# The first expert layer of nineteen late slots, computed from quarter blocks with seven products

## The chip, the cores and the metric

The kernel runs on one core of one Trainium2 chip. The metric is the device time of one execution in microseconds; 893.2 us is the median of seven runs before the change (892.81 to 895.32). The core has five engines with a queue each: PE (matrix products, with its weight loads shown apart as PEld), DVE (vector), ACT (activation), POOL (GpSimd) and SP (issues transfers). All arithmetic is in 32-bit floats.

## The reference

A layer norm, a cross attention with 16 heads onto 64 context rows per batch, a gated residual, a second layer norm, and a mixture of 8 experts of which each of the 4096 tokens uses two:

```python
x = x + tanh(g_xattn) * attention(layernorm(x), ctx, ctx)
# the experts, on xt = layernorm(x), 4096 x 256
logits = einsum('td,ed->te', xt, gate_w)
w_topk, sel = top_k(logits, 2)
combine = zeros((T, E)).at[arange(T)[:, None], sel].add(softmax(w_topk))
h = silu(einsum('td,edf->tef', xt, w1))      # first layer, 256 -> 1024
y = einsum('tef,efd->ted', h, w2)            # second layer, 1024 -> 256
x = x + tanh(g_ffn) * einsum('ted,te->td', y, combine)
```

## The kernel before, in words

The attention runs over eight groups of 512 tokens. After the second layer norm every token is written twice, once for each chosen expert, into a table in device memory that is sorted by expert. The experts are then computed in "slots": a slot is a stretch of table rows of one expert. Nine early slots (0 to 8, `NA` = 9) take rows of the first four groups and run while the attention of the rest goes on. Late slots begin at 9. The first eight of them (9 to 16, `NW` = 8) are three blocks of 128 rows wide, so 384 rows; the others (17 on) have two blocks, 256 rows. This execution computes slots 0 to 29.

`run_slots` is the loop over slots. For slot `s` it runs `hidden` (L842: the first layer), then `transposed` for slot `s + 1` (L832: DVE turns the rows into columns, `xT`), then `combine` (L942: the second layer) of slot `s - 1`, then `quarter_sums` of slot `s` (L878), and asks for the weights of slot `s + 3` and the rows of slot `s + 4`. So the second layer runs one slot behind the first. In what follows "a first-layer stretch" is the time in which PE computes `hidden` of one slot, and "a second-layer stretch" that of `combine`.

`hidden` multiplies, for each of eight feature blocks of 128, two halves of the 256 inputs (`NC` = 2) by all rows of the slot: 16 products with 384 or 256 columns, added up in PSUM. One instruction of ACT then applies silu to 768 or 1024 columns of PSUM and writes `hT`. DVE has no part in it.

The second layer of slots 9 to 27 (`by_quarters`, L875) is already computed with seven products in place of eight on two by two quarter blocks (a scheme of Strassen and Winograd). `quarter_sums` makes eight sums of 128 x 512 on DVE, four of `hT` and four of `w2`, all with both inputs in SBUF. `pair_of_blocks` (L898) has seven products of four 128 x 128 matmuls and leaves PSUM through ACT (L923, L933) and DVE (L918). A third block is computed the plain way (L987). The scaled rows are added to the output by an indirect transfer that POOL issues (`scatter`, L958).

Names that matter: `block` gives out buffers of 8 KB per partition in three shares, "group" (8), "weight" (7) and "hidden" (2). `w1` and `w2` of even late slots counted from 9 lie in "weight", those of odd ones in "group"; `sh` and `sw` lie in "weight"; `hT` lies in "hidden", or for every second wide slot in "group". `ps2` is two tiles of two PSUM banks each, used by `hidden`; `ps1` is four banks, used by the second layer. `soft` with the tag "pr" is two tiles of 1024 columns. `kept` are the eight residual tiles of the attention; the first two of them are not used by late slots.

The order of instructions on each engine is not that of the source alone: a scheduler at build time issues what it holds to be ready, earlier source first, and each engine then works through its queue strictly in order.

Of the kernel before, what the change touches and what calls it, by code (L numbers as in the profile page):

```python
# [8 lines left out]
F32 = mybir.dt.float32  # L9
I32 = mybir.dt.int32  # L10
AF = mybir.ActivationFunctionType
ALU = mybir.AluOpType
# [3 lines left out]
P = 128  # L16
# [5 lines left out]
def kernel(  # L22
# [36 lines left out]
    nc = tc.nc  # L59
# [3 lines left out]
    H, _, DK = w_qs.shape  # L63
    E, _, F = w1.shape
# [6 lines left out]
    NC = D // P  # L71
    NF = F // P
# [5 lines left out]
    NA = -(-(2 * HG * G - E * (S - 1)) // S)  # L78
# [12 lines left out]
    soft = ctx.enter_context(tc.tile_pool(name="soft", bufs=2))  # L91
# [5 lines left out]
    ps2 = ctx.enter_context(tc.tile_pool(name="ps2", bufs=2, space=PSUM))  # L97
    ps1 = ctx.enter_context(tc.tile_pool(name="ps1", bufs=4, space=PSUM))

    def block(shape, name, share):  # L100
        return blocks.tile(shape, F32, tag=share, bufs=shares[share], name=name)

    def bank(name, spare=False):

        if spare:
            return ps2.tile([P, 2, 512], F32, tag="ps2", name=name)[:, 0]
        return ps1.tile([P, 512], F32, tag="ps1", name=name)
# [3 lines left out]
    of = out.rearrange("b l d -> (b l) d").rearrange("(g t p) d -> g p t d", p=P, t=T)  # L111
# [10 lines left out]
    kept = [const.tile([P, T * RW], F32, tag=f"x{g}", name=f"x{g}") for g in range(NG)]  # L122
# [38 lines left out]
    wk, _ = next(load_wk)  # L161
# [603 lines left out]
    def is_wide(s):  # L765
        return NA <= s < NA + NW
# [15 lines left out]
    def load_tokens(s):  # L782

        blocks = 3 if is_wide(s) else 2
        ids = routed.tile([P, 3, 2, 2], F32, tag="ids", name=f"ids_{s}")[:, :blocks]
        xin = places(s)
        parts = [(1, 0, 2), (2, 2, 3)][: blocks - 1]
        behind = ["cleared", "table0"] if s < NA else ["cleared", "table0", "table1"]
        assert entered >= (HG if s < NA else NG) * T * 2
        for row, first, last in parts:  # L790
            n = (last - first) * P
            with behind_loads():
                r = number(s, row, table_rows - n)
            of = table[bass.ds(r, n), :]
            load = nc.sync.dma_start(
                ids[:, first:last, 0], of[:, 0:2].rearrange("(t p) c -> p t c", p=P)
            )
            apart("table", load, behind=behind)
            with tc.issue_after(load.ins):
                load = nc.sync.dma_start(  # L800
                    ids[:, first:last, 1], of[:, D + 2 : D + 4].rearrange("(t p) c -> p t c", p=P)
                )
            apart("table", load, behind=behind)
            for c in range(P // Q):
                with tc.issue_after(load.ins):
                    load = nc.sync.dma_start(
                        xin[c * Q : (c + 1) * Q, first:last].rearrange("j t (i w) -> j (t i) w", w=D // 4),
                        of[:, 2 + c * (D // 4) : 2 + (c + 1) * (D // 4)].rearrange("(i j) w -> j i w", j=Q),
                    )
                apart("table", load, behind=behind)  # L810
            issued[:] = [load.ins]
        return ids, xin

    def load_weights(s):

        with behind_loads():
            e = number(s, 0, E - 1)
        w = s - NA
        share = "weight" if s < NA or w % 2 == 0 else "group"
        a = block([P, NC, F], f"w1_{s}", share)  # L820
        nc.sync.dma_start(a, w1[bass.ds(e, 1)].rearrange("o (p c) f -> p (o c) f", p=P))
        b = block([P, NF, D], f"w2_{s}", share)
        issued[:] = [
            nc.sync.dma_start(b, w2[bass.ds(e, 1)].rearrange("o (c p) d -> p (o c) d", p=P)).ins
        ]
        return a, b
# [5 lines left out]
    def transposed(s, xin):  # L832
        blocks = xin.shape[1]
        pool, tag = (rows, "xT") if blocks == 2 else (npool, "nT")
        xT = pool.tile([P, NC, blocks * P], F32, tag=tag, name=f"xT_{s}")
        nc.vector.transpose(
            xT.rearrange("p c (i j) -> p i c j", j=Q),
            xin.rearrange("p t (i m c) -> p (t i) c m", c=NC, m=Q),
        )
        return xT  # L840

    def hidden(s, a, xT):  # L842

        n = xT.shape[2]
        if is_wide(s):
            share = "hidden" if (s - NA) % 2 == 0 else "group"
            hT = [block([P, NF // 2, n], f"hT_{s}_{i}", share) for i in range(2)]
        else:
            hT = [block([P, NF, n], f"hT_{s}", "hidden")]
        per_tile = NF // len(hT)  # L850
        step = 4 if attention_ends and not is_wide(s) else 2
        for f0 in range(0, NF, step):
            if not attention_ends:
                ph = bank(f"ph_{s}_{f0}").rearrange("p (i n) -> p i n", i=2)
            elif is_wide(s):
                ph = ps2.tile([P, 2, 512], F32, tag="ps2", name=f"ph_{s}_{f0}")[:, :, :n]
            else:
                ph = ps2.tile([P, step, n], F32, tag="ps2", name=f"ph_{s}_{f0}")
            for i in range(step):
                f = f0 + i  # L860
                for c in range(NC):
                    nc.tensor.matmul(  # L862
                        ph[:, i, :],
                        a[:, c, f * P : (f + 1) * P],
                        xT[:, c, :],
                        start=(c == 0),
                        stop=(c == NC - 1),
                    )
            f1 = f0 % per_tile
            nc.scalar.activation(hT[f0 // per_tile][:, f1 : f1 + step, :], ph, AF.Silu)  # L870
            yield hT

    attention_ends = False

    def by_quarters(s):  # L875
        return NA <= s < NA + OFTEN - 2
# [126 lines left out]
    def run_slots(slots):  # L1003

        ahead = 3
        issued.clear()
        tokens, weights = {}, {}

        def load(s):
            if s in slots:  # L1010
                weights[s] = load_weights(s)

        def load_next(s):
            if s in slots:
                tokens[s] = load_tokens(s)

        for s in slots[:ahead]:
            load(s)
            load_next(s)
        load_next(slots[0] + ahead)  # L1020
        yield
        yield
        xT = transposed(slots[0], tokens[slots[0]][1])
        yield
        pending = None
        for s in slots:
            a, b = weights.pop(s)
            ids, xin = tokens.pop(s)
            if s == slots[-1] and pending:
                yield from combine(*pending)  # L1030
                pending = None
            for hT in hidden(s, a, xT):
                yield
            if s + 1 in slots:
                xT = transposed(s + 1, tokens[s + 1][1])
                yield
            if pending:
                yield from combine(*pending)
            pending = (s, ids, b, xin, hT, quarter_sums(s, b, hT) if by_quarters(s) else None)
            load(s + ahead)  # L1040
            load_next(s + ahead + 1)
        yield from combine(*pending)
# [64 lines left out]


    slots = run_slots(range(NA + OFTEN))
    pieces = {HG + 2: (0, 0, 1, 1), HG + 3: (3, 3, 2, 2), HG + 4: (3, 3, 3, 3)}  # L1110
    last = None
# [13 lines left out]
    for g in range(NG + 1):  # L1125
# [7 lines left out]
        for t in range(T):  # L1133
            if t == 0 and g >= 2:
                leave(g - 2)
            if g < NG:
                pr = probabilities(g, t, qT)
# [44 lines left out]
    for _ in slots:  # L1182
# [3 lines left out]
    _, used = nc.values_load_multi_w_load_instructions(  # L1186
        in_use[0:1, 0:1], min_val=0, max_val=NB, bass_reorder=False
    )
    with tc.If(used[0] > OFTEN):
        for _ in run_slots(range(NA + OFTEN, NA + RARELY)):  # L1190
            pass
        with tc.If(used[0] > RARELY):
            for _ in run_slots(range(NA + RARELY, NS)):
                pass
# [32 lines left out]
```

## Time and profile before

| | |
|---|---|
| median of seven runs | 893.2 us |
| the profiled execution's own time | 893.94 us |
| its span, first to last instruction | 892.2 us |
| busy: PE, DVE, ACT, POOL | 856.0, 451.7, 250.7, 259.8 us |
| first layer of all slots on PE (L862) | 248.1 us |
| second layer by quarters on PE (L908) | 134.4 us (54.0 + 40.1 + 20.2 + 20.1) |
| sums of `quarter_sums` on DVE (L895) | 103.5 us |
| mean granted clock of PE | 0.986 |

The span is what the profile shows between the first and the last instruction; 1.7 us of the execution's own time lie around it. The slots that the change touches are computed between about 542 and 868 us of the span. A matmul of 32-bit floats shows as two records: the 16 products of `hidden` are 32 records per slot. Start times are the best measure of PE's pace, as the ends of matmuls are modelled.

### The profile page before, as it was taken

What the parts mean: (1) busy time and instruction counts of PE and PEld (TensorE: products, weight loads), DVE (VectorE), ACT (ScalarE), POOL (GpSimd) and SP (SyncE); (2) the same over time, 40 slices, a digit from 0 to 9 for tenths busy, and PEclk for the clock granted to TensorE, in tenths of its full rate; (3) what the DMA queues carried; (4) which work ended last, traced back from release to release, by engine and by line L of the source; (5) the groups of instructions that cost most, each with busy time, mean ns of one, the idle gap of its engine ahead of it and who ended that gap; (6) DMA issues with size and microseconds to landing.
All of it is one profiled execution on the core that took longest, in us unless ns stands there. A gap on an engine that the chain in (4) does not pass through costs nothing. (4 is left out here: it accounts for less than half of the span.)

```text
span 892.2 us, 13019 instructions
## 1 busy us (share of the span) xinstructions
PE 856.0 (96%) x4632; PEld 668.1 (75%) x4632; DVE 451.7 (51%) x1073; ACT 250.7 (28%) x391; POOL 259.8 (29%) x207
## 2 busy tenths in 40 slices
PE   6999999999999997999999899999999999999995
PEld 4565858585857667685888587777777999999994
DVE  4366384669565966662138111454333546546430
ACT  2573252534243224440132011222122112212210
POOL 3042212123711371107214521312222232222132
PEclk9999999999999999898999899999999999999998
DMA  9999997001100155327576687774554846887421
GB/s 199 339 340 341 340 345 220 20 1 59 60 24 1 42 168 146 106 58 215 143 201 154 180 208 172 188 188 122 136 164 85 226 101 168 218 238 222 115 24 23
DMA packets 163254, 140.56 MB, mean 158 GB/s; under 512 B 72944, under 2 KB 157296, under 8 KB 159344
## 3 DMA queue, kind: packets, MB, share of 16 engines
q1 hardware_dynamic: 143728, 117.84, 45.5%
q0 software_dynamic: 12864, 16.86, 10.0%
q10 hardware_dynamic: 6592, 4.98, 1.7%
q8 instruction: 38, 0.62, 0.3%
q14 instruction: 32, 0.26, 0.1%
HBM read 80.76 MB, written 59.41 MB: 157 GB/s over the span
## 5 line engine op out<-in xcount | busy, mean ns | idle before, releaser
L862 PE MATMUL ph<-xT,w 128*128 128x256 f32 (+1 forms) x960 | 248.1, 414 | 4.4 <-issue 4.3
L862 PEld LDWEIGHTS ph<-xT,w 128*128 128x128 f32 x960 | 182.7, 193 | 59.0 <-issue 9.4
L958 POOL DMA_INDIRECT out_dram<-x,ids x68 | 111.5, 1639 | 328.1 <-DVE x L918 197.1
L870 ACT ACTIVATE hT<-ph 128x1024 f32<-128x1024 f32 (+2 forms) x80 | 71.0, 896 | 286.1 <-PE ph L862 241.4
L421 POOL TENSOR_TENSOR pr<-pr,sm 128x1024 f32<-128x1024 f32 x32 | 61.3, 1917 | 233.3 <-DVE sm L419 173.8
L387 PE MATMUL pq<-nT_a,wq 128*128 128x512 f32 x256 | 116.0, 596 | 6.7 <-DVE qT L455 4.7
L463 PE MATMUL pp<-wp,qT 128*128 128x256 f32 x512 | 113.1, 379 | 0.0
L463 PEld LDWEIGHTS pp<-wp,qT 128*128 128x128 f32 x512 | 97.1, 190 | 18.2 <-issue 5.5
L987 PE MATMUL py<-w,hT 128*128 128x256 f32 x480 | 107.6, 381 | 0.0
L987 PEld LDWEIGHTS py<-w,hT 128*128 128x128 f32 x480 | 91.1, 191 | 12.4
L387 PEld LDWEIGHTS pq<-nT_a,wq 128*128 128x128 f32 x256 | 46.2, 190 | 59.4 <-issue 44.5
L583 POOL DMA_INDIRECT table<-x,to_row x64 | 62.6, 978 | 42.4 <-DVE x L572 21.2
L402 PEld LDWEIGHTS sc<-keys,qT 128*128 128x128 f32 x512 | 62.9, 193 | 12.0 <-issue 11.6
L402 PE MATMUL sc<-keys,qT 128*128 128x128 f32 x512 | 67.4, 279 | 0.0
L971 DVE TENSOR_SCALAR x<-py,ids 128x256 f32<-128x256 f32 x30 | 14.5, 482 | 102.3 <-PE py L987 89.8
L432 ACT COPY aT<-pa 128x512 f32<-128x512 f32 x64 | 34.9, 590 | 83.0 <-PE pa L431 72.9
L908 PE MATMUL q<-sw,sh 128*128 128x128 f32 x456 | 54.0, 275 | 0.0
L908 PEld LDWEIGHTS q<-sw,sh 128*128 128x128 f32 x456 | 52.5, 192 | 0.3
L411 DVE TENSOR_REDUCE mx<-sc 128x16 f32<-128x1024 f32 x32 | 39.0, 1218 | 26.7 <-PE sc L402 26.5
L418 DVE TENSOR_REDUCE sm<-pr 128x16 f32<-128x1024 f32 x32 | 38.9, 1217 | 19.8 <-ACT pr L416 18.7
L455 DVE TENSOR_TENSOR qT<-po,qT 128x512 f32<-128x512 f32 x64 | 41.0, 678 | 14.1 <-PE po L446 11.8
L394 ACT COPY qT<-pq 128x512 f32<-128x512 f32 x64 | 36.2, 580 | 34.4 <-PE pq L387 33.8
(198 smaller groups left out, 853.4 us busy)
## 6 DMA issues: line engine op xcount, KB each, us to landing
w<-in_L_ffn_w_dram SPq DMA_DIRECT2D x60, 1024.0 KB
table<-empty SPq DMA_DIRECT2D x8, 4620.0 KB
x<-table SPq DMA_DIRECT2D x120, 64.0 KB
out_dram<-x ACTq DMA_DIRECT2D x8, 512.0 KB
x<-in_x_dram SPq DMA_DIRECT2D x7, 512.0 KB
out_dram<-x,ids POOLq DMA_INDIRECT x68
wq<-in_L_xattn_w_qs_dram SPq DMA_DIRECT2D x4, 256.0 KB
wv<-in_L_xattn_w_vs_dram SPq DMA_DIRECT2D x2, 512.0 KB
```

The costliest lines, as they stand in the source:

```text
L387: nc.tensor.matmul(pq, wq[:, c, p * P : (p + 1) * P], nT[g][:, c, :], start=(c == 0), stop=(c == NC - 1),)
L402: nc.tensor.matmul(sc[:, p // 2, :, p % 2, :], of_pair(qT, p)[:, t * P : (t + 1) * P], kT[g // GB][:, p, :], start=True, stop=True,)
L411: nc.vector.tensor_reduce(mx, scv, AX.X, ALU.max)
L421: nc.gpsimd.tensor_tensor(pr, pr, sm.unsqueeze(2).to_broadcast([P, H, M]), ALU.mult).ins
L455: nc.vector.tensor_tensor(own, po[j], own, ALU.mult)
L463: nc.tensor.matmul(pp[:, i, :], of_pair(qT, p)[:, t * P : (t + 1) * P], wp[:, p, :], start=(p == 0), stop=(p == NP - 1),)
L583: nc.gpsimd.indirect_dma_start(out=table.rearrange("r (u w) -> (r u) w", w=2), out_offset=bass.IndirectOffsetOnAxis(ap=to_row[:, k, i : i ...
L862: nc.tensor.matmul(ph[:, i, :], a[:, c, f * P : (f + 1) * P], xT[:, c, :], start=(c == 0), stop=(c == NC - 1),)
L870: nc.scalar.activation(hT[f0 // per_tile][:, f1 : f1 + step, :], ph, AF.Silu)
L908: nc.tensor.matmul(to, left[:, f, :], right[:, f, :], start=not onto and f == 0, stop=f == NF // 2 - 1, skip_group_check=onto,)
L958: rows_added = nc.gpsimd.indirect_dma_start(out=outf[:n], out_offset=bass.IndirectOffsetOnAxis(ap=of_rows[:, t, 0, 1:2], axis=0), in_=y[:, t],
L987: nc.tensor.matmul(py[t], hT[f // per_tile][:, f % per_tile, t * P : (t + 1) * P], b[:, f, :], start=(f == 0), stop=(f == NF - 1),)
```

## The change

The first layer of slots 9 to 27 is computed from quarter blocks as well: the rows of a slot are cut into two halves (192 rows in wide slots, 128 in the others), the features into two halves of 512, and the inputs are already in two halves. Seven products take the place of eight. Each product is, per feature block, one matmul of 128 x 128 weights by 192 or 128 columns.

- `first_sums` makes four sums of `w1` on POOL, each 128 x 512, into a new block `sa` of the share "group", and four sums of `xT` on DVE into `kept[0]` or `kept[1]`.
- `hidden_by_quarters` runs the products. `per` is 512 divided by the half's rows: two feature blocks at a time in wide slots (so two rounds), all four in the others (one round). Each round takes both tiles of `ps2`. ACT copies the first product to `u2`; DVE adds five times, each time one PSUM and one SBUF input; ACT applies silu four times, three of these in place on `hT`.
- `run_slots` calls `first_sums` of slot `s + 1` right after `transposed` of it.

```diff
+    def first_by_quarters(s):
+        return by_quarters(s)
+
+    def first_sums(s, a, xT):
+
+        half = NF // 2 * P
+        sa = block([P, 4, half], f"sa_{s}", "group")
+        w = [[a[:, c, f * half : (f + 1) * half] for c in range(NC)] for f in range(2)]
+        h = xT.shape[2] // 2
+        sx = kept[(s + 1) % 2][:, : 4 * h].rearrange("p (q n) -> p q n", n=h)
+        x = [[xT[:, c, t * h : (t + 1) * h] for t in range(2)] for c in range(NC)]
+        for engine, out_, in0, in1, op in (
+            (nc.gpsimd, sa[:, 0], w[1][0], w[1][1], ALU.add),
+            (nc.gpsimd, sa[:, 1], sa[:, 0], w[0][0], ALU.subtract),
+            (nc.gpsimd, sa[:, 2], w[0][0], w[1][0], ALU.subtract),
+            (nc.gpsimd, sa[:, 3], w[0][1], sa[:, 1], ALU.subtract),
+            (nc.vector, sx[:, 0], x[0][1], x[0][0], ALU.subtract),
+            (nc.vector, sx[:, 1], x[1][1], sx[:, 0], ALU.subtract),
+            (nc.vector, sx[:, 2], x[1][1], x[0][1], ALU.subtract),
+            (nc.vector, sx[:, 3], x[1][0], sx[:, 1], ALU.subtract),
+        ):
+            engine.tensor_tensor(out_, in0, in1, op)
+        return w, x, sa, sx
+
+    def hidden_by_quarters(s, n, sums):
...
+        per = 512 // h
+        for f0 in range(0, NF // 2, per):
+            banks = [ps2.tile([P, 2, 512], F32, tag="ps2", name=f"ph_{s}_{f0}_{i}") for i in range(2)]
+            q = [banks[i // 2][:, i % 2, : per * h].rearrange("p (f n) -> p f n", n=h) for i in range(4)]
+            u = soft.tile([P, 2, per * h], F32, tag="pr", name=f"u_{s}_{f0}")
...
+            def product(to, left, right, onto=False):
+                for f in range(per):
+                    nc.tensor.matmul(
+                        to[:, f, :],
+                        left[:, (f0 + f) * P : (f0 + f + 1) * P],
+                        right,
...
+                    )
+
+            def plus(to, of, other):
+                nc.vector.tensor_tensor(to, of, other, ALU.add)
+
+            def leave_hidden(f, t, of=None):
+                nc.scalar.activation(to[f][t], to[f][t] if of is None else of, AF.Silu)
+
+            product(q[0], w[0][0], x[0][0])
+            nc.scalar.copy(u2, q[0])
+            product(q[1], sa[:, 1], sx[:, 1])
+            plus(u2, q[1], u2)
+            product(q[2], sa[:, 2], sx[:, 2])
+            plus(u3, q[2], u2)
+            product(q[3], sa[:, 0], sx[:, 0])
+            plus(to[1][1], q[3], u3)
+            leave_hidden(1, 1)
+            product(q[0], w[0][1], x[1][0], True)
+            leave_hidden(0, 0, q[0])
+            product(q[2], w[1][1], sx[:, 3], True)
+            plus(to[1][0], q[2], u2)
+            leave_hidden(1, 0)
+            product(q[3], sa[:, 3], x[1][1], True)
+            plus(to[0][1], q[3], u2)
+            leave_hidden(0, 1)
+            yield hT
...
-            for hT in hidden(s, a, xT):
+            for hT in hidden_by_quarters(s, xT.shape[2], first) if first else hidden(s, a, xT):
                 yield
+            first = None
             if s + 1 in slots:
                 xT = transposed(s + 1, tokens[s + 1][1])
+                if first_by_quarters(s + 1):
+                    first = first_sums(s + 1, weights[s + 1][0], xT)
                 yield
```

More of the change, by code (lines that the diff above doesn't have):

```diff
@@ new lines, in hidden_by_quarters @@
+    def hidden_by_quarters(s, n, sums):
+        w, x, sa, sx = sums
+        h = n // 2
+        if is_wide(s):
+            share = "hidden" if (s - NA) % 2 == 0 else "group"
+            hT = [block([P, NF // 2, n], f"hT_{s}_{i}", share) for i in range(2)]
+            halves_of = hT
+        else:
+            hT = [block([P, NF, n], f"hT_{s}", "hidden")]
+            halves_of = [hT[0][:, i * NF // 2 : (i + 1) * NF // 2] for i in range(2)]
+        per = 512 // h
[3 more added lines that the diff above has]
+            u = soft.tile([P, 2, per * h], F32, tag="pr", name=f"u_{s}_{f0}")
+            u2, u3 = (u[:, i].rearrange("p (f n) -> p f n", n=h) for i in range(2))
+            to = [[halves_of[f][:, f0 : f0 + per, t * h : (t + 1) * h] for t in range(2)] for f in range(2)]
+            def product(to, left, right, onto=False):
[4 more added lines that the diff above has]
+                        right,
+                        start=not onto and f == 0,
+                        stop=True,
+                        skip_group_check=onto or f > 0,
+                    )
[21 more added lines that the diff above has]
+            yield hT
@@ L1024, in run_slots @@
         yield
-        pending = None
+        pending = first = None
         for s in slots:
```

## The prediction

> **What bounds the kernel now.** I read the page's busy line first, then stages, then the order on PE, then the other engines' rows in the same stretches. The page's first part:
>
> ```profile
> PE 856.0 (96%) x4632; PEld 668.1 (75%) x4632; DVE 451.7 (51%) x1073; ACT 250.7 (28%) x391; POOL 259.8 (29%) x207
> ```
>
> A mean over the span hides the stages, so the windows (PE, PEld, DVE, ACT, POOL busy, then granted clock, DMA share, GB/s):
>
> ```profile
> 400.00:450.00 50.00, 48.26 (x215) 37.54 (x215) 12.68 (x36) 3.41 (x5) 21.85 (x20) 0.93 0.60 169
> ...
> 650.00:700.00 50.00, 50.00 (x261) 38.61 (x260) 20.83 (x48) 10.46 (x17) 13.26 (x8) 1.00 0.50 129
> ...
> 750.00:800.00 50.00, 50.00 (x341) 47.02 (x340) 28.82 (x67) 11.03 (x20) 13.27 (x8) 1.00 0.76 208
> 800.00:850.00 50.00, 50.00 (x342) 47.01 (x341) 26.64 (x62) 11.37 (x20) 11.66 (x7) 1.00 0.57 154
> ```
>
> In the late slots PE has no idle time at a full clock, and every other engine is far from full. PE's work is the bound there, and a microsecond taken from it is a microsecond of the time, as long as nothing else becomes the bound. PE in order of time (start, length, records):
>
> ```profile
> 660.33 10.48 PE L862 MATMUL ph<-xT,w 128*128 128x384 f32 x32
> 670.65 1.05 PE L908 MATMUL q<-w,hT 128*128 128x128 f32 x8
> ...
> 795.95 7.07 PE L862 MATMUL ph<-xT,w 128*128 128x256 f32 x32
> 802.86 1.05 PE L908 MATMUL q<-w,hT 128*128 128x128 f32 x8
> 803.75 2.84 PE L908 MATMUL q<-sw,sh 128*128 128x128 f32 x24
> ...
> 809.11 7.07 PE L862 MATMUL ph<-xT,w 128*128 128x256 f32 x32
> ```
>
> Start to start, the first layer takes 10.32 us in a wide slot (322.5 ns per record) and 6.91 us in a two-block slot (215.9 ns). The second layer's 56 records take 6.25 us (111.6 ns). A two-block slot is 13.16 us (795.95 to 809.11); a wide slot adds a third block of 16 records and is 20.03 us (640.30 and 660.33 are starts of the same place).
>
> **The gain on PE.** Seven products of four matmuls are 56 records. In two-block slots they have 128 columns: 56 x 111.6 ns = 6.25 us, 0.66 less. In wide slots they have 192 columns, which no row shows. On the line through 256 and 384 columns one is 162.6 ns, midway between 128 and 256 it is 163.8; with 163 the stretch is 9.13 us, 1.19 less (both ends within 0.04). Sum: 11 x 0.66 + 8 x 1.19 = 16.8 us. [...]
>
> **What is added beside PE.** Rows by form (busy, mean ns, then idle before):
>
> ```profile
> L455 DVE TENSOR_TENSOR qT<-po,qT 128x512 f32<-128x512 f32 x64 | 41.0, 678 | 14.1 <-PE po L446 11.8 <-PE pq L387 1.0 <-remote 0.7
> ...
> L895 DVE TENSOR_TENSOR sw<-w 128x512 f32<-128x512 f32 x38 | 25.8, 683 | 0.0
> ...
> L421 POOL TENSOR_TENSOR pr<-pr,sm 128x1024 f32<-128x1024 f32 x32 | 61.3, 1917 | 233.3 <-DVE sm L419 173.8 <-ACT qT L394 18.4 <-DVE mv_b L276 11.9
> ...
> L870 ACT ACTIVATE hT<-ph 128x512 f32<-128x512 f32 x8 | 4.6, 596 | 3.4 <-PE ph L862 3.4
> ```
>
> ACT: a copy and four silus of 512 columns, 5 x 0.6 = 3.0 us, where two of 1024 columns took 2.05. Its 11 us in 50 become some 15. Cost nothing: PE's own stretch hides it; without that cover it is 1 us a slot.
>
> DVE, two-block slots: (28.82 + 26.64) / 7.6 slots = 7.3 us now. Five additions out of PSUM have the form of L455: 0.68 each, 0.60 when queued closely, so 3.2 us. Four sums of 128 columns are not in the trace; the nearest rows are 0.345 us (L918, 128 columns) and 0.22 us (64 columns, L525 at its shortest): I take 0.28, 1.1 us, with 0.9 and 1.4 as ends. Sum 11.6 us in a slot for which PE would need 12.50. Wide slots: 20.83 / 2.5 = 8.3 now, ten additions of 384 columns (0.55 down to 0.47 by the same row) 5.1, sums 1.3: 14.7 of 18.84. So DVE alone still fits, but in two-block slots with 0.9 us to spare, and it is now in PE's loop: the sixth product may start once the second addition has read its bank, the seventh once the third has. Queue by queue, counted from the start of a first-layer stretch: products end every 0.89 us; additions follow 0.2 us later and take 0.68, so the second ends by 3.6 where the sixth product wants 4.46. About 0.9 us of lateness is free there, and 0.9 to 1.0 at the same two places of the second layer. What stands before those additions in DVE's queue are the eight sums of `quarter_sums`, earlier in the source. They run from 804.12 to 809.7 in the slot shown; with the last silu now some 1.2 us after the last product (0.2 + 0.68 + 0.6, against 1.2 for one silu of 1024) they end hardly later, so the first addition, due 2.0 us into the stretch, meets a free DVE.
>
> POOL: four sums of 128 x 512 from the row of 1917 ns for 1024 columns: 0.95 us each (ends 0.9 and 1.2), 3.9 a slot, beside two or three issues of 1.6. It has the room, 7.3 of 12.5 us. Its scatters may come up to 3.9 us later, and nothing waits for them soon. The weights' transfers start early enough for the sums:
>
> ```profile
> 755.77 0.36 SPq L821 DMA_DIRECT2D w<-in_L_ffn_w_dram  x1
> ...
> 762.80 0.36 SPq L821 DMA_DIRECT2D w<-in_L_ffn_w_dram  x1
> ```
>
> These are for slots 23 and 24, whose first layers began at 782.79 and 795.95, 27 and 33 us later; 1 MB at the 300 to 400 GB/s of these microseconds lands in some 5. `sa` takes one or two of the eight "group" buffers, of which two late pairs use four: no load is late by this, and a whole slot (13 us) of delay would still be hidden.
>
> **The wait I weigh most.** POOL's sums and DVE's sums meet. The trace has a few such meetings in the attention:
>
> ```profile
> 305.72 1.90 POOL L421 TENSOR_TENSOR pr<-pr,sm 128x1024 f32<-128x1024 f32 x1 [11.20 <-DVE past_a L613]
> 305.76 1.93 DVE L619 TENSOR_TENSOR terms_a<-before,past_a 1x64 f32<-1x64 f32 x1
> ...
> 378.76 1.90 POOL L421 TENSOR_TENSOR pr<-pr,sm 128x1024 f32<-128x1024 f32 x1 [7.29 <-DVE sm L419]
> 379.77 0.91 DVE L947 TENSOR_TENSOR ids<-ids 128x2 int32<-128x2 int32 x1 [1.18 <-DMA ids<-table]
> ```
>
> A DVE sum of 64 numbers that takes 0.21 us elsewhere took 1.93, and one of two numbers 0.91 for 0.15: both end when POOL's instruction ends. The L455 at 171.03, with one input in PSUM, took 0.63 beside a running L421. So DVE's instructions with two SBUF inputs stand still for the rest of a POOL sum. [...] By that rule the five additions are exempt, the twelve sums are not; a sum without it would keep the 16.8 us.
>
> What it costs depends on where the four POOL sums fall. Below: none meets, 0. Above: all four meet the sums fully, 4 x 0.95 = 3.8 us of DVE per slot. The eight sums fill 5.6 of 13.16 us. By the loads above, POOL's sums of one slot could begin near 761 (in a first-layer stretch, running 2 us into the next second-layer stretch), those of the other near 768 (in the last microsecond and a half of a second-layer stretch). I take two of four, 0.7 us each, so 1.4. Then a two-block slot needs 11.6 + 1.4 = 13.0 us of DVE: DVE takes over from PE, and of 0.66 only 0.16 is left. A wide slot needs 16.1 of 18.84, so PE stays the bound, with some local lateness beyond the free 0.9: I keep 0.9 of 1.19. Sum: 11 x 0.16 + 8 x 0.9 = 9.0 us. The profiled execution's own 893.94 becomes 884.9; it lies 0.7 above the median of 893.2, and I say 885.
>
> **Rivals.** *All of it arrives*: POOL's sums fall into first-layer stretches, where DVE mostly has exempt work; 893.2 - 16.8 = 876.4. For it: 9 us of each slot in which POOL is free; against: the buffer of `sa` comes free just when a second-layer stretch starts. *Nothing measurable*: between two and two and a half sums meet, two-block slots lose 0.3 to 0.4 (11 x 0.4 = 4.4), wide ones keep 0.5 (4.0): 893. *Slower*: DVE is the bound in two-block slots because three or four POOL sums meet its sums. Three at full length: 11.6 + 2.85 = 14.45, 1.3 over 13.16, 14.2 us; wide ones keep 0.4, 3.2: 904. Four: 15.4, 24.6 us, wide ones at zero: 918. The point from which two-block slots lose is 13.16 - 11.6 = 1.6 us of blocking; overall it is 2.2, with the wide gain of 7. PE's new gaps could add to it: in the window from 400 to 450 above, PE was 96.5% busy and its clock 0.93. Two-block slots last 145 us in all; at 0.93 that alone is 10.
>
> **How the numbers follow.** Partial gain (880 to 890) 0.40, all of it 0.12, nothing 0.12, slower 0.36. The likeliest case gives 885. The low end is the full gain, 876.5; the high end is the rival with three meetings, 905, which leaves out about 0.15. About 0.2% (1.8 us) can be told from no change: faster 0.52, same 0.12, slower 0.36.
>
> **What would show it.** First layer: 56 records start to start in 6.25 us (two-block) and 9.1 us (wide); longer means waits, and the waits of PE would name DVE's additions. DVE's busy share from 750 to 850 should rise from 55% to above 90%, with rows of L895's forms well above 683 ns where POOL's new sums run. If those rows stay at 683 ns the blocking is refuted and the time should be near 877. If wide slots are not faster, my picture of DVE's slack is wrong; if PE waits for ACT or a transfer, none of these cases holds.

## The result, and the profile after

The changed kernel takes 988.3 us (median of 19 runs), the kernel before 893.1 us (46 runs). The ratio is 1.107, with a 95% interval from 1.105 to 1.109. The forecast was 885 us in a range of 876.5 to 905: a small gain, where the kernel became 95 us slower. The profiled execution after has a span of 980.5 us at a mean clock of 0.958 (before: 892.2 at 0.986).

The page's busy line after:

```profile
PE 878.1 (90%) x5088; PEld 719.2 (73%) x5088; DVE 610.1 (62%) x1284; ACT 276.3 (28%) x472; POOL 369.2 (38%) x283
```

From it comes an account of the 88.3 us by which the span grew. PE's idle time is span less busy: 36.2 us before, 102.4 after, so 66 more. PE's busy time rose by 22 us, where the products should have taken 16.8 less; so 39 us went into longer records. So 66 + 39 - 16.8 = 88. The granted clock explains at most 29 of the 39: the span times one less the clock is 12.5 us before and 41.2 after. The ends of matmuls are modelled, so the other ten may be short waits within the busy time; no run here tells. The windows of the late slots (PE, PEld, DVE, ACT, POOL busy, granted clock, DMA share, GB/s):

```profile
650.00:700.00 50.00, 43.13 (x276) 39.71 (x274) 40.27 (x71) 13.36 (x30) 24.82 (x17) 1.00 0.51 121
750.00:800.00 50.00, 42.17 (x334) 40.69 (x333) 42.77 (x70) 11.56 (x23) 27.20 (x19) 0.96 0.58 139
800.00:850.00 50.00, 42.99 (x320) 41.41 (x320) 42.78 (x78) 10.64 (x21) 29.68 (x19) 0.87 0.46 126
```

PE, which had no idle microsecond here, is idle for 7 to 8 of 50, and in the last window its clock is 0.87. DVE is busy for 40 to 43 of 50, with only 70 to 78 instructions. What ended PE's idle time from 530 us on (us in total, times, longest; before, PE has no wait there):

```profile
PE q L987 <- DVE sw L974: 27.0, 10, 7.9
PE ph L918 <- DVE hT L928: 17.0, 9, 5.0
PE ph L918 <- DVE u L928: 14.3, 7, 4.1
PE ph L918 <- POOL sa L894: 5.7, 3, 4.4
```

All but the last of these four name DVE: its sums for the second layer (L974) and its additions in the first (L928). These three rows are 58.3 of 66.7 us; short waits not shown here add 2.7. The groups by form show why (busy us, mean ns, idle before; the first line is from the kernel before):

```profile
L895 DVE TENSOR_TENSOR sw<-w,sw 128x512 f32<-128x512 f32 x38 | 25.9, 681 | 0.0
...
L974 DVE TENSOR_TENSOR sw<-w,sw 128x512 f32<-128x512 f32 x38 | 40.5, 1065 | 0.0
L974 DVE TENSOR_TENSOR sw<-w 128x512 f32<-128x512 f32 x38 | 35.1, 949 | 0.0
...
L894 POOL TENSOR_TENSOR sa<-w 128x512 f32<-128x512 f32 x38 | 56.9, 1730 | 7.1 <-PE ph L918 7.1
```

DVE's sums, 681 and 683 ns before, average 1065 and 949. One place in the timeline shows how (start, us):

```profile
794.53 5.20 DVE L974 TENSOR_TENSOR sw<-w,sw 128x512 f32<-128x512 f32 x1
...
794.90 3.06 POOL L894 TENSOR_TENSOR sa<-w 128x512 f32<-128x512 f32 x2
...
797.34 1.83 POOL L894 TENSOR_TENSOR sa<-sa,w 128x512 f32<-128x512 f32 x1
799.25 1.61 POOL L894 TENSOR_TENSOR sa<-w,sa 128x512 f32<-128x512 f32 x1
799.66 0.68 DVE L928 TENSOR_TENSOR u<-ph,u 128x512 f32<-128x512 f32 x1
800.26 2.02 DVE L894 TENSOR_TENSOR x<-xT 128x128 f32<-128x128 f32 x2
800.39 1.78 PEld L918 LDWEIGHTS ph<-x,sa 128*128 128x128 f32 x8 [4.28 <-DVE u L928]
800.39 2.08 PE L918 MATMUL ph<-x,sa 128*128 128x128 f32 x8 [4.09 <-DVE u L928]
```

One DVE sum, otherwise 0.68 us long, took 5.20 us: it stood through three POOL sums, which end at 799.17, and ended 0.56 us later, at 799.73. Behind it in DVE's queue waited the addition L928. That addition has one input in PSUM and ran in 0.68 us although a POOL sum ran beside it, so it is not shut out itself; but it is late, and PE waited 4.09 us for it. After this gap PE's eight records take 2.08 us, where eight such records took 1.05 us before: the clock had fallen (0.50 from 800.39 to 802.26). It fell within the gap, which runs from 796.30 to 800.39: the granted clock is 1.00 from 796.30 to 798.80, 0.63 from there to 799.30, and 0.50 from 799.30 to the gap's end. So it was halved 2.6 us into this gap, and in experiment 6 below the records behind a gap of 3.15 us were slow as well.

### The profile page after: what moved, and what is told of

Its sections match the earlier page's. It is cut to its first block, busy times and chain, and to the rows that moved or that the text cites. A ratio compares the mean times of both kernels' runs of the same rounds, so it can differ in the third digit from the quotient of the medians.

```text
span 980.5 us, 14410 instructions
## 1 busy us (share of the span) xinstructions
PE 878.1 (90%) x5088; PEld 719.2 (73%) x5088; DVE 610.1 (62%) x1284; ACT 276.3 (28%) x472; POOL 369.2 (38%) x283
## 5 line engine op out<-in xcount | busy, mean ns | idle before, releaser
L918 PE MATMUL ph<-x,sa 128*128 128x128 f32 (+1 forms) x456 | 80.7, 318 | 20.2 <-DVE u L928 12.2
L987 PE MATMUL q<-sw,sh 128*128 128x128 f32 x456 | 73.4, 308 | 27.0 <-DVE sw L974 27.0
L862 PE MATMUL ph<-xT,w 128*128 128x256 f32 x352 | 85.8, 395 | 4.1 <-issue 3.8
L987 PEld LDWEIGHTS q<-sw,sh 128*128 128x128 f32 x456 | 67.7, 222 | 28.9 <-DVE sw L974 28.9
L918 PEld LDWEIGHTS ph<-x,sa 128*128 128x128 f32 x456 | 67.5, 204 | 24.9 <-DVE u L928 12.9
L931 ACT ACTIVATE hT<-hT 128x384 f32<-128x384 f32 (+1 forms) x81 | 45.8, 566 | 138.0 <-DVE hT L928 138.0
L928 DVE TENSOR_TENSOR hT<-ph,u 128x384 f32<-128x384 f32 (+1 forms) x81 | 49.4, 610 | 55.4 <-PE ph L918 51.9
L862 PEld LDWEIGHTS ph<-xT,w 128*128 128x128 f32 x352 | 68.0, 197 | 18.3 <-issue 9.3
L402 PEld LDWEIGHTS sc<-keys,qT 128*128 128x128 f32 x512 | 62.9, 193 | 12.0 <-issue 11.6
L894 POOL TENSOR_TENSOR sa<-w 128x512 f32<-128x512 f32 x38 | 56.9, 1730 | 7.1 <-PE ph L918 7.1
L918 PE MATMUL ph<-xT,w 128*128 128x128 f32 (+1 forms) x304 | 53.4, 309 | 3.3 <-DVE u L928 2.1
```

Of the source, the lines that this page charges most:

```text
L402: nc.tensor.matmul(sc[:, p // 2, :, p % 2, :], of_pair(qT, p)[:, t * P : (t + 1) * P], kT[g // GB][:, p, :], start=True, stop=True,)
L862: nc.tensor.matmul(ph[:, i, :], a[:, c, f * P : (f + 1) * P], xT[:, c, :], start=(c == 0), stop=(c == NC - 1),)
L894: engine.tensor_tensor(out_, in0, in1, op)
L918: nc.tensor.matmul(to[:, f, :], left[:, (f0 + f) * P : (f0 + f + 1) * P], right, start=not onto and f == 0, stop=True, skip_group_check=on ...
L928: nc.vector.tensor_tensor(to, of, other, ALU.add)
L987: nc.tensor.matmul(to, left[:, f, :], right[:, f, :], start=not onto and f == 0, stop=f == NF // 2 - 1, skip_group_check=onto,)
```

## The experiments

Theory A: POOL's sums shut out DVE's sums with two SBUF inputs, and what stands behind these, additions included, stops PE. Theory B: it is DVE's load and the order in its queue, whatever POOL does. Theory C: the sums of `xT` go to a buffer that early slots' scatters still read, and this wait (`DVE x L894 <- DMA out_dram<-x,ids`, 21.4 us in four waits) upsets what follows. Each ratio is against the kernel before, run beside it on the same chip: 892.0 us for experiments 1 to 4, 896.2 for 5 to 8, 897.8 for 9 to 11 and 879.3 for 12.

### 1. POOL writes only

```diff
-            (nc.gpsimd, sa[:, 0], w[1][0], w[1][1], ALU.add),
...
+        for i in range(4):
+            for part in range(3):
+                nc.gpsimd.memset(sa[:, i], 0.0)
```

> The changed kernel, but POOL fills the four weight sums with zeros (three memsets of 128 x 512 for each, so POOL is busy about as long) and reads nothing; the first layer's products are computed with these zeros, so the output isn't the reference's. Theory A (POOL's sums read SBUF and shut out DVE's instructions with two SBUF inputs for the whole run of four, 5.6 us, and everything behind them waits): rows of quarter_sums fall back to 683 ns, the longest from 5.2 us to under 1 us, and the time falls from 988 to between 870 and 905. Rival B (DVE has too much to do and its additions stand behind its sums in the queue; POOL has no part in it): at least 950. Rival C (the loss is one wait at the start, for the scatters of the early slots to leave the tiles that the input sums go into): at least 960.

Measured: 914.7 us, 1.025 (1.022 to 1.028). The page's busy line, and the group of the sums (now at L973):

```profile
PE 858.5 (94%) x5088; PEld 702.4 (77%) x5088; DVE 548.0 (60%) x1284; ACT 276.2 (30%) x472; POOL 380.3 (42%) x435
```

```profile
L973 DVE TENSOR_TENSOR sw<-w,sw 128x512 f32<-128x512 f32 x38 | 25.9, 681 | 0.0
```

The sums of `w1` are left out here, `sa` holds zeros. POOL is busier than in the changed kernel (380 against 369 us), but reads nothing; DVE's sums are back at 681 ns. The same 1284 instructions of DVE take 548.0 us in place of 610.1. So 62.1 us, 3.3 us a slot, were DVE standing still beside POOL's sums. Without that the time falls by 8.2% of before, 73 us; 2.5% remain. That is 10 us above A's range and 35 below the least that B gave. The queues hardly changed with it: all but 16 of DVE's 1284 instructions and all but 158 of PE's 5088 records stand in the same order in both traces, so it is not a new order that gives the time back.

### 2. All sums on DVE

```diff
-            (nc.gpsimd, sa[:, 0], w[1][0], w[1][1], ALU.add),
+            (nc.vector, sa[:, 0], w[1][0], w[1][1], ALU.add),
```

The other three sums likewise.

> The changed kernel with the four weight sums moved from POOL to DVE. Theory A: nothing shuts DVE out, but it has 4 x 0.6 = 2.4 us more per slot: 14.0 us in two-block slots (0.85 over the 13.16 of before, so 11 x 0.85 = 9 us lost), 17.1 of 18.84 in wide ones (8 x 1.19 = 9.5 us won): 885 to 915. Rival B: DVE is more loaded than in the changed kernel, so slower than it, 990 or more. Rival C: 980 to 990 as in the changed kernel.

Measured: 916.9 us, 1.028 (1.025 to 1.031). Windows:

```profile
750.00:800.00 50.00, 47.42 (x413) 46.40 (x413) 47.01 (x106) 14.17 (x30) 13.41 (x7) 1.00 0.75 199
800.00:850.00 50.00, 47.07 (x403) 45.54 (x401) 47.61 (x106) 15.05 (x31) 16.00 (x8) 1.00 0.78 205
```

DVE does four more sums of 0.68 us a slot and is nearly full in the two-block slots, and still the time is 71 us below the changed kernel's. That separates A from a mere load on DVE. The time lies 2 us above A's range, and the remaining 2.8% fit a share of B.

### 3. POOL's sums alone, in the kernel before

```diff
             if s + 1 in slots:
                 xT = transposed(s + 1, tokens[s + 1][1])
+                if by_quarters(s + 1):
+                    weight_sums(s + 1, weights[s + 1][0])
                 yield
```

`weight_sums` holds the four POOL sums of `first_sums`; nobody reads them.

> The kernel before, with the plain first layer, and beside it the four weight sums on POOL in slots 9 to 27, which nobody reads. Only the blocking is added: DVE's queue has 5.9 us to spare in a two-block slot, but the weighting of the second layer stands behind the blocked sums. Theory A: a run of four sums (5.6 us) holds one DVE sum for up to 5 us, of which about 1 is free for PE: 905 to 960. Rivals B and C: 893, within 3 us.

Measured: 901.3 us, 1.010 (1.004 to 1.017). The busy line, and PE's waits from 530 us on:

```profile
PE 854.2 (95%) x4632; PEld 668.2 (74%) x4632; DVE 506.3 (56%) x1073; ACT 250.7 (28%) x391; POOL 361.2 (40%) x283
```

```profile
PE q L921 <- DVE q L931: 8.5, 7, 2.6
```

This is the run that says most. DVE's 1073 instructions take 506.3 us in place of 451.7: 54.6 us of standing still, nearly as much as in the changed kernel, with the same instructions in the same order on PE, DVE and ACT as before. Yet it costs only some 9 us, less than A expected and more than its rivals did. In the kernel before, a first-layer stretch needs nothing of DVE, so 5 to 10 us of PE's work at a time cover DVE's lateness. The change puts five or ten additions of DVE into that stretch and takes the cover away. Blocking alone costs 9, the new form without blocking 23 (experiment 1), both together 95. The blocked sums are not the same ones, though:

```profile
L908 DVE TENSOR_TENSOR sh<-hT 128x512 f32<-128x512 f32 x30 | 53.9, 1801 | 36.1 <-ACT hT L870 36.1
...
567.12 11.40 DVE L908 TENSOR_TENSOR sh<-hT 128x512 f32<-128x512 f32 x1
```

Some 33 of the 54.6 us fall on these sums behind a silu (20.5 us in all before), where in the changed kernel 25 of 62 fall on those of `w2`. So it is shown that the amount of blocking alone does not set the price; that the lost cover makes the difference, and not the place of the blocking, is argued.

### 4. Wide slots alone, sums on POOL

```diff
     def first_by_quarters(s):
-        return by_quarters(s)
+        return is_wide(s)
```

> The changed kernel with quarter blocks in the first layer of the eight wide slots alone, sums on POOL as there. Theory A: wide slots are hit too (DVE 14.7 + up to 5.6 of 18.84 us, and the free lateness is 1 us): 900 to 945. Rival B: DVE fits into wide slots, so their gain stays: 882 to 888. Rival C: the whole loss is at the start of the wide slots, so 970 or more.

Measured: 935.5 us, 1.049 (1.041 to 1.056). Wide slots lose as well, some 5 us each, though the prediction gave DVE 4 us to spare in each of them.

### 5. The sums of xT in the slot's own rows

```diff
-        sx = kept[(s + 1) % 2][:, : 4 * h].rearrange("p (q n) -> p q n", n=h)
+        sx = xin.rearrange("p t d -> p (t d)").rearrange("p (q n) -> p q n", n=h)
```

> The changed kernel, but the sum over the four blocks of x (sx) is written into the slot's own rows tile, which is dead after the transpose, instead of a buffer that the early slots' scatters still read. Theory A (POOL's run of four sums shuts out VectorE's sums for the whole run): the main loss stays; only the waits on the scatters of out_dram (21 us in all by the trace, partly behind other work) go: 968 to 984 us. Theory C (the one-time wait of sx is a main cause of the loss): under 960 us. Theory B (the load of VectorE alone, whoever else works): 980 to 992 us, for no sum is taken from VectorE.

Measured: 1002.9 us, 1.118 (1.113 to 1.124): no faster at all, and above the ranges of all three theories. Its busy line:

```profile
PE 886.2 (89%) x5088; PEld 728.2 (73%) x5088; DVE 626.4 (63%) x1284; ACT 276.2 (28%) x472; POOL 368.6 (37%) x283
```

DVE's waits for the scatters are gone from the trace, but its instructions now stand still for 626.4 - 548.0 = 78 us in place of 62. The wait was there, and taking it away gave no time back. As the blocking rose with it, experiment 7 has to say what the wait alone is worth.

### 6, 7, 8. All sums on DVE, own rows: wide slots, all 19, two-block slots

> Seven products in the eight three-block slots alone, all sums on VectorE and none on POOL, sx in the slot's own rows tile. Theory A with C: nothing is left that stops VectorE, so the gain on TensorE arrives: 893 minus 8 times 1.19 = 9.5, 880 to 890 us. Theory B (more sums on VectorE push the additions behind them and hold TensorE's buffers): 895 to 915 us.

> All 19 slots with seven products, all sums on VectorE, sx in the slot's own rows tile. Without the last change this took 916.9 us, with waits of 16.9 us on the early scatters. Theory C: 898 to 908 us. Theory B (VectorE's queue is full in the two-block slots, 95 per cent busy there): the two-block slots keep their loss, 905 to 917 us.

> Seven products in the eleven two-block slots alone, all sums on VectorE, sx in the slot's own rows tile. Theory B (these slots are bound by VectorE, which has 14.2 us of work in a slot where TensorE has 12.5 and had 13.2): 11 times 0.5 to 1.3 us above before, 898 to 908 us. Rival (VectorE's load is spread over the neighbours and TensorE's gain arrives): 893 minus 11 times 0.66 = 7, 884 to 890 us.

The three kernels join the edits of experiments 2 and 5; for two-block slots alone the condition is `by_quarters(s) and not is_wide(s)`.

Measured: wide slots 908.9 us, 1.014 (1.010 to 1.018); all 917.1, 1.023 (1.016 to 1.029); two-block slots 900.6, 1.005 (1.002 to 1.009). The two parts add up to the whole (1.4 + 0.5% against 2.3%, within the intervals). All fell on B's side (experiment 7 at the upper edge of its range). Experiment 7 repeats experiment 2 without the wait on the scatters, and its time is the same within the intervals, 1.023 against 1.028: theory C falls. In the wide-slot run, PE in order of time:

```profile
565.89 0.38 PE L987 MATMUL q<-w,hT 128*128 128x128 f32 x2
569.42 3.57 PE L987 MATMUL q<-sw,sh 128*128 128x128 f32 x16 [3.15 <-DVE sw L974]
...
627.57 0.81 PE L918 MATMUL ph<-x,sa 128*128 128x192 f32 x4
628.22 0.61 PE L987 MATMUL q<-sw,hT 128*128 128x128 f32 x4
```

and DVE ahead of the gap:

```profile
565.67 0.69 DVE L974 TENSOR_TENSOR sh<-hT,hT 128x512 f32<-128x512 f32 x1 [0.59 <-ACT hT L931]
...
568.69 0.68 DVE L974 TENSOR_TENSOR sw<-w,sw 128x512 f32<-128x512 f32 x1
569.29 0.68 DVE L974 TENSOR_TENSOR sw<-w 128x512 f32<-128x512 f32 x1
```

The eight sums begin behind the last silu at 565.67 and follow one another each 0.60 us. PE has the inputs it needs only after the sixth of them, and no first-layer stretch is left to run in between, because the products of both layers have been set in turn on PE. The sixteen records after the gap take 3.4 us (569.42 to 572.83, at a granted clock of 0.53) in place of 1.8; from 540 to 580 us the clock is 0.96. The lower two lines give the price of a record of 192 columns: 0.65 us for four, 162.5 ns each. Windows of the same run:

```profile
580.00:620.00 40.00, 33.36 (x183) 31.25 (x182) 29.39 (x60) 10.22 (x22) 6.43 (x4) 0.87 0.43 104
620.00:660.00 40.00, 39.28 (x260) 37.11 (x260) 34.34 (x76) 12.34 (x28) 9.59 (x6) 1.00 0.63 149
```

The loss lies in the first slots of the new form; from 620 us on PE is nearly always busy.

### 9. POOL's sums with gaps

```diff
             (nc.gpsimd, sa[:, 0], w[1][0], w[1][1], ALU.add),
+            (nc.gpsimd, sa[:, 1], None, None, None),
             (nc.gpsimd, sa[:, 1], sa[:, 0], w[0][0], ALU.subtract),
...
+            if in0 is None:
+                engine.memset(out_, 0.0)
+            else:
+                engine.tensor_tensor(out_, in0, in1, op)
```

A fill stands ahead of the second, third and fourth sum.

> The changed kernel with a fill of the next 128 x 512 block (which reads nothing) between POOL's sums, so that they do not follow one another directly. POOL's work per slot grows by three fills. Theory A1 (it is the unbroken run of four sums that keeps VectorE out, and VectorE gets in wherever POOL runs something that does not read): the longest sum of L974's kind falls from 5.2 to 1.5 to 2.5 us, and the time to 930 to 965 us. Theory A2 (every POOL sum costs VectorE its own length, wherever it stands): the rows of these sums keep their total, 980 to 1000 us.

Measured: 987.5 us, 1.099 (1.091 to 1.107). The sums, now L980 (min/median/max ns, first and last start):

```profile
L980 DVE TENSOR_TENSOR sw<-w x38: 677/684/2778, 581.6 to 950.3; 128x512 f32<-128x512 f32 x38
L980 DVE TENSOR_TENSOR sw<-w,sw x38: 675/683/3105, 582.8 to 950.9; 128x512 f32<-128x512 f32 x38
```

The longest sum falls from 5.2 to 3.1 us, so gaps do let DVE in sooner. DVE's busy time hardly changes: 608.5 us, 60.5 above experiment 1's. And the time stays. A2's forecast came true: in this pair of runs the sum of all meetings goes with the time, and the 5.20 us row above is only their most visible form.

### 10, 11, 12. Later start, and the sums of w2 first

```diff
     def first_by_quarters(s):
-        return is_wide(s)
+        return is_wide(s) and s >= NA + 2
```

```diff
+            early = w2_sums(s, b) if first else None
             for hT in hidden_by_quarters(s, xT.shape[2], first) if first else hidden(s, a, xT):
...
-            pending = (s, ids, b, xin, hT, quarter_sums(s, b, hT) if by_quarters(s) else None)
+            pending = (s, ids, b, xin, hT, quarter_sums(s, b, hT, early) if by_quarters(s) else None)
```

`w2_sums` holds the four sums of `w2` out of `quarter_sums`. Both edits start from experiment 6; experiment 12 has both.

> As the run with the wide slots alone, VectorE's sums and the slot's own rows, but seven products only from slot 11 on, so in six slots. In that run PE stood still 10.8 us between 540 and 620 us of the span and ran its next records at a slower pace, and lost nothing after 620. Theory R (the loss belongs to the entry into the new form, where the second layer by quarters has nothing else beside it, whichever slot comes first): the same loss at a later place, 905 to 912 us. Theory P (the loss belongs to slots 9 and 10, where other work is done as well): the loss goes and six gains of some 1.2 us stay, 883 to 891 us.

> As the run with the wide slots alone, VectorE's sums and the slot's own rows, but the four sums of w2 are issued ahead of the slot's first layer, and not behind its last silu. Theory B (order in VectorE's queue: eight sums of 0.60 us behind the last silu, for which PE waited 3.2 us twice, and additions behind sums): most of the waits go, 884 to 897 us. Theory that VectorE's amount of work decides, whatever its order: 903 to 912 us.

> Both last changes together: seven products in slots 11 to 16 alone, all sums on VectorE, and the sums of w2 issued ahead of the first layer. If the waits for L974 that were left (2.7 us) and the slower records behind them go, some 4 to 7 us of the 7.5 us of work taken from TensorE arrive: 886 to 892 us beside a kernel before at 893. If what is left is the crossing of first- and second-layer products and additions in VectorE's queue, it stays within 3 us of before.

Measured: from slot 11 on 897.7 us, 0.9995 (0.996 to 1.003); `w2` first 904.6, 1.007 (1.004 to 1.011); both 877.3 beside 879.3 for the kernel before on that chip, 0.9977 (0.9968 to 0.9986). PE's waits from 530 us on, in the first of the three and in the last:

```profile
PE q L987 <- DVE sw L974: 2.7, 2, 1.4
PE q L987 <- ACT q L1002: 1.4, 2, 0.7
```

```profile
PE q L996 <- DVE sh L983: 2.3, 3, 1.1
```

Taking the four sums of `w2` from behind the silu, with no work removed, halves the loss of experiment 6 (1.4% to 0.7%, with intervals that just touch): that half is order, not load. It is less than theory B expected, and the 904.6 us lie in the range given for the amount of work (903 to 912), so what the other half is stays open. For slots 9 and 10, P was nearer than R, since the loss did not come back at a later place; but the gain of six slots did not arrive either. The last kernel is 2.0 us faster than before (0.1 to 0.3%), 7.1 us being the work it saves PE (6 x 1.19); that is the second case of its forecast, within 3 us of before. Two-block slots stay as they were.

## Why the prediction was wrong

**PE's pace was right.** 192-column records take 162.5 ns start to start (163 predicted). Records of 128 columns take the 111 ns that were assumed, where the clock is full (the group of eight at 795.02 us in the trace after is followed by the next at 795.91).

**The length of a POOL sum was too small.** "0.95 us each (ends 0.9 and 1.2)" came from a form of 1024 columns. The shortest sums of 128 x 512 take 1.27 us (runs in the trace have starts 1.22 to 1.28 us apart), above the upper end.

**The step that failed is the blocking:** "I take two of four, 0.7 us each, so 1.4". Experiment 1 measures 3.3 us a slot, close to the upper bound of 3.8. By the prediction's own sum this gives 11.6 + 3.3 = 14.9 us of DVE in a two-block slot, 1.74 over 13.16, 19 us in eleven; wide slots would still fit with 18.0 of 18.84. So even the right size would have forecast about 910, and 78 us would be missing.

**The larger error is the model behind that sum:** "So DVE alone still fits", DVE's work per slot against PE's. DVE's own work was sized well: 82.7 of 100 us busy from 750 to 850 in experiment 1, at 13.8 us a slot (by the starts of its transposes), are 11.4 us, against 11.6. Yet those slots need 13.8 us where PE has work for 12.5. With 83% of load DVE's queue still made PE wait: 11.3 of the 19.7 us of PE's waits in experiment 1 name DVE's sums and additions. "The first addition, due 2.0 us into the stretch, meets a free DVE" took the two layers for separate stretches. In the trace the products of both alternate on PE, and on DVE additions stand behind sums. In experiment 3, with that cover in place, nearly as much blocking costs 9 us. One reading was off here too: of the eight sums said to run from 804.12, the first ran at 800.71, inside the first-layer stretch.

**The clock was named, but too small:** 10 us as an addition to the slower rival; up to 29 us by the granted clock, so up to 0.4 us more for each microsecond of new gap (29 to 66).

**What the prediction did not have:** the wait of `sx` for the scatters. By experiments 5 and 7 it is no cause of the loss. Loads and ACT were rightly costed at next to nothing: no wait of PE names a transfer in the late slots, and 2.0 us name ACT. The rule that the prediction drew from the attention's meetings held in kind, but not in length: a DVE sum stood still not for the rest of one POOL sum, but through several that followed one another directly, three at 794.53 and eight in experiment 3. How often they meet, and what would stand behind the blocked sums, was guessed. That additions with an input in PSUM are exempt rested on the row at 171.03, which had begun 0.26 us before the POOL sum; the row at 799.66 above, begun inside one and 0.68 us long, shows it. Of the signs it named, DVE's sums did rise well above 683 ns and wide slots were not faster; DVE's share from 750 to 850 reached 86%, not 90.

The nearest rival was "four meetings", 918: the right mechanism, with a price that left out cover and clock. The joint 63 us (95 less 9 less 23) can be split only roughly. PE's waits from 530 us on are 66.7 us in the changed kernel, 19.7 in experiment 1 and 9.0 in experiment 3, so 38 of the 63 are PE standing still. The span times one less the clock is 41 us, 17 and 10, with 13 before, so at most 26 are the clock; no run here holds it fixed. Which of the crossed orders of first- and second-layer products keeps the last few microseconds of experiments 10 to 12 was not tried either.

## What to carry to other kernels

Before adding steps of another engine into the loop of the one that bounds the kernel, ask what that loop was covering. The stretch that needed no DVE was, by the account above, PE's store against every lateness of DVE, and it was worth more than the products saved. A sum placed on POOL because POOL has room is not free if DVE makes sums with two SBUF inputs beside it: price every meeting (here about 0.8 us of DVE for each POOL sum). And busy shares added up per slot don't show a queue's order: look at what stands ahead of the instruction that the bounding engine will wait for.

## What the runs showed of the hardware

A DVE sum with two SBUF inputs can stand through several POOL sums, not just the rest of one: 5.20 us through three of them at 794.53, and 11.40 us through eight (567.58 to 577.96) at 567.12 in experiment 3. Both ended 0.56 us behind the last of these sums. A few microseconds later, from 800.26, DVE's small sums did come through between POOL's, three in 2.02 and 1.35 us. Gaps without reads brought the longest down to 3.1 us but left the total at 60 us: about 0.8 us of DVE for each of 76 POOL sums. That POOL loses as well is not shown: its records, 1.27 us at their shortest, average 1.48 to 1.73 us by form, but they overlap, and the starts of those eight stay 1.22 us apart. Beside POOL's fills of 128 x 512 in experiment 1 DVE's sums took 681 to 692 ns by form, as in the kernel before (681 to 693). And after gaps of 3.15 and 4.09 us on PE the next records ran at half the pace: eight in 2.08 us for 1.05, sixteen in 3.4 for 1.8.
